# Row means of a binarized weight: reduced from its own layout on VectorE and spread through memory, in place of a product with ones

## The chip, the core and the metric

One core of one Trainium2 chip. The metric is the device time of one execution in microseconds (us), the median over several executions. The engines in the profile are PE (TensorE; PEld is its weight load), DVE (VectorE), ACT (ScalarE), POOL (GpSimd) and SP (SyncE, which here issues nearly all DMA transfers, in a fixed order).

## The reference, cut to what matters

A gated recurrence over 4096 time steps with a residual and a layer norm, then a feed-forward layer with binarized weights, a residual and a second layer norm. Only the second weight of the feed-forward layer is touched:

```python
# w1: (1024, 256)   w2: (256, 1024)   x: (2, 4096, 256)
def _binarize(w):
    alpha = mean(abs(w), axis=1, keepdims=True)
    return alpha * sign(w)          # forward value
h   = gelu(einsum('bsd,hd->bsh', x, _binarize(w1)) + b1)
out = einsum('bsh,dh->bsd', h, _binarize(w2)) + b2
```

So alpha of w2 is one number for each of the 256 output columns: the mean of the absolute values of 1024 weights. The kernel multiplies by the signs alone, and scales each output column by its alpha afterwards.

## The kernel before

The 4096 steps of each of the two sequences are cut into 64 segments of 64 steps that run side by side, each with 40 warm-up steps taken from the segment before it. One recurrence step is then one product of a 128x128 weight with 128 columns (`steps`, L165, PE) and one tanh (L170, ACT), and these steps follow one another strictly. The other work comes in 16 chunks of 512 rows: gates (L331), mix (L392, L399 to L407), projection (L417, L428), first layer norm, the two feed-forward products `up` (L514) and `down` (L563), second layer norm and store.

The whole order of work is written out by hand: within `tc.manual_schedule` each engine, SP included, runs its instructions in program order. Before the loop over chunks there is a start-up part, `for p in range(48)`: each `p` runs a part of the gates and lets a recurrence step in; `VISITS` puts in the products that make u (L138), which need the x tiles loaded by `load_xT` (L104); `AROUND` says after which `p` a load or a preparation of a weight is issued. `load_w(2)` and `load_w(3)` (p = 22 and 30) load the two halves of w2, `prepare_w(2)` and `prepare_w(3)` (p = 34 and 42) prepare them.

The layout of w2 in the chip is that of its transpose: `w2T` has h on the partitions (8 groups of 128) and the 256 output columns d in a row. `prepare_w` takes one half of it (4 groups) and does two things on DVE:

- the absolute values are summed over the 4 groups in one `tensor_reduce` through a rearranged view, 1024 values in and 256 sums out for each partition (L231); after the second half the two results are added (L239);
- the signs are formed (`signs`, L203 and L204) into `sg2`, the operand of `down`.

What is left is a sum over the 128 partitions. `mean_w2` (L246 to L250) does it after the start-up part, with one product of a 128x128 matrix of ones and the 256 sums (L248, PE). This also leaves the total in all 128 partitions, where `scale` (L579) needs it. DVE takes it out of PSUM with the factor 1/1024 into `al2_r` (L249). It uses a buffer `h` of pool `p_1` (three, shared with the gates' and `up`'s results), and `al2` takes one of three `hlo` buffers.

`mean_w2` stands right after the transposes of chunk 0 (`do(0, "turn", True)`) and ahead of `mix_end` of chunk 2, `norm` of chunk 1 and the last start-up gates. The first use of `al2_r` is `scale` of chunk 0, in the loop's round c = 1.

SP's order around these places is: ... x tile 2, half 2 of `w2T`, x tiles 3 and 4, half 3 of `w2T`, x tile 5, then the loads that chunks 0 to 2 need (`hu` from the state, `xn` from x, L364, L368, L373), then for chunk 3 `hu` (L364), an x tile for chunk 6 (L356), the other half of `hu` (L368) and `xn` (L373). After those come sixteen small transfers `xlo<-xb` for each chunk from 2 on (L480), which finish a transpose.

Of the kernel before, what the change touches and what calls it, by code (L numbers as in the profile page):

```python
# [8 lines left out]
FP = mybir.dt.float32  # L9
# [3 lines left out]
ALU = mybir.AluOpType  # L13
AX = mybir.AxisListType
PSUM = bass.MemoryType.PSUM

P = 128
B, T, DM, S, H = 2, 4096, 256, 64, 1024
KD = DM // P
# [4 lines left out]
N = 512  # L24
# [13 lines left out]
def gated_recurrence_then_binary_ffn(  # L38
# [9 lines left out]
    b_out: bass.AP,  # L48
    w1: bass.AP,
    w1T: bass.AP,  # L50
    w2T: bass.AP,
    b2: bass.AP,
    out: bass.AP,
):
    nc = tc.nc

    cp = ctx.enter_context(tc.tile_pool(name="const", bufs=1))
    xp = ctx.enter_context(tc.tile_pool(name="xin", bufs=2))
    wk = ctx.enter_context(tc.tile_pool(name="work", bufs=2))
    sm = ctx.enter_context(tc.tile_pool(name="small", bufs=4))  # L60
    p_s = ctx.enter_context(tc.tile_pool(name="p_s", bufs=1, space=PSUM))
    p_m = ctx.enter_context(tc.tile_pool(name="p_m", bufs=1, space=PSUM))
    p_1 = ctx.enter_context(tc.tile_pool(name="p_1", bufs=3, space=PSUM))
# [19 lines left out]
    b1_c = bias_c[:, 1 + KD :]  # L83
    bg_c = cp.tile([P, KD], FP, name="bg_c")
    al1 = cp.tile([P, KH], FP, name="al1")
    al2 = wk.tile([P, 2, DM], FP, tag="hlo", name="al2", bufs=3)
    bo_r = cp.tile([P, DM], FP, name="bo_r")
    b2_r = cp.tile([P, DM], FP, name="b2_r")
    al2_r = cp.tile([P, DM], FP, name="al2_r")
    ident = cp.tile([P, P], FP, name="ident")  # L90
    ones = cp.tile([P, P], FP, name="ones")
# [107 lines left out]
    def signs(dst, src, nm):  # L199

        for i in range(2):
            neg = wk.tile([P, N], FP, tag="xlo", name=f"neg{nm}_{i}")
            nc.vector.tensor_scalar(neg, src[:, bass.ts(i, N)], 0.0, None, ALU.is_lt)  # L203
            nc.vector.scalar_tensor_tensor(  # L204
                dst[:, bass.ts(i, N)], src[:, bass.ts(i, N)], 0.0, neg, ALU.is_gt, ALU.subtract
            )

    w_tiles = {}

    def load_w(n):  # L210
        half = bass.ts(n % 2, KH // 2)
        if n < 2:
            t = wk.tile([P, H], FP, tag="h", name=f"w1t{n}")
            nc.sync.dma_start(out=t, in_=w1T[:, n, :])
            t2 = wk.tile([P, KH // 2, DM], FP, tag="xhi", name=f"w1n{n}")
            nc.sync.dma_start(out=t2, in_=w1[:, half, :])
            w_tiles[n] = t, t2
        else:
            t = wk.tile([P, KH // 2, DM], FP, tag="h", name=f"w2t{n}")
            nc.sync.dma_start(out=t, in_=w2T[:, half, :])  # L220
            w_tiles[n] = t, None

    def prepare_w(n):
        half = bass.ts(n % 2, KH // 2)
        t, t2 = w_tiles[n]
        if n < 2:
            nc.vector.tensor_reduce(al1[:, half], t2, AX.X, ALU.add, apply_absolute_value=True)
            nc.vector.tensor_scalar(al1[:, half], al1[:, half], 1.0 / DM, None, ALU.mult)
            signs(sg1[:, n, :], t, f"a{n}")
        else:  # L230
            nc.vector.tensor_reduce(  # L231
                al2[:, n % 2, :],
                t.rearrange("p j d -> p d j"),
                AX.X,
                ALU.add,
                apply_absolute_value=True,
            )
            if n == 3:
                nc.vector.tensor_add(al2[:, 0, :], al2[:, 0, :], al2[:, 1, :])  # L239
            signs(  # L240
                sg2[:, half, :].rearrange("p j d -> p (j d)"),
                t.rearrange("p j d -> p (j d)"),
                f"b{n}",
            )

    def mean_w2():  # L246
        ps = p_1.tile([P, N], FP, tag="h", name="ps_al2")
        nc.tensor.matmul(ps[:, :DM], ones, al2[:, 0, :], start=True, stop=True)  # L248
        nc.vector.tensor_scalar(al2_r, ps[:, :DM], 1.0 / H, None, ALU.mult)  # L249
        yield  # L250


    class Stats:
# [430 lines left out]
    def ready():  # L684
        return done < len(plan) and plan[done] // SPC in have_u

    def next_steps():
        nonlocal done
        done += 1
        steps(plan[done - 1], done == WARM)  # L690
        for i in range(3):
            if done == WARM + (i + 1) * SPC:
                ch[i].load_h()
        if waiting and not held:
            for what, args in waiting:
                what(*args)
            waiting.clear()

    def emit(what, pieces, pace=5600):
        nonlocal since  # L700
        for _ in pieces:
            since += COST.get(what, 0)
            if since >= pace:
                since = min(since - pace, pace // 2)
                if ready():
                    next_steps()
# [5 lines left out]
    def do(i, what, *args, pace=5600):  # L712
        if not 0 <= i < len(ch):
            return
        if what == "load_h":
            need = WARM + (ch[i].c + 1) * SPC
            while done < need:
                next_steps()
            ch[i].load_h()
        elif what in ("load_u", "load_n", "load_x", "load_gate_x"):  # L720
            getattr(ch[i], what)()
        else:
            emit(what, getattr(ch[i], what)(*args), pace)
# [4 lines left out]
    def parts(n, pace):  # L728
# [10 lines left out]
        3: [(load_xT, 12), (load_xT, 13)],  # L739
        6: [(load_xT, 14)],  # L740
        8: [(load_w, 0)],
        11: [(load_xT, 15), (load_xT, 0)],
        13: [(load_weights,)],
        15: [(load_w, 1)],
        17: [(load_xT, 1)],
        18: [(prepare_w, 0)],
        20: [(load_xT, 2)],
        22: [(load_w, 2)],
        23: [(halve_weights,)],
        26: [(load_xT, 3), (load_xT, 4)],  # L750
        28: [(prepare_w, 1)],
        30: [(load_w, 3), (load_xT, 5)],
        34: [(prepare_w, 2)],
        36: [(ch[0].load_u,), (ch[1].load_n,)],
        40: [(ch[1].load_u,), (ch[2].load_u,)],
# [5 lines left out]
    with tc.manual_schedule(engines={ET.PE, ET.Activation, ET.DVE, ET.Pool, ET.SP}):  # L761
# [40 lines left out]
            next_steps()  # L802
        waiting = None
        do(0, "turn", True)
        emit("", mean_w2())
        mixed = ch[2].mix_end()
        next(mixed)
        do(1, "norm", nc.vector)
# [182 lines left out]
```

## Time and profile before

| | us |
|---|---|
| median of 3 runs (432.11, 432.14, 433.4) | 432.14 |
| time of the profiled execution | 432.98 |
| span from its first to its last instruction | 431.2 |
| first product of the start-up part's last visit to u (L138) | 52.63 |
| `mean_w2`'s product starts (L248) | 83.82 |
| `scale` first reads `al2_r` (L579) | 112.2 |

The mean granted clock of TensorE is 0.995 of full speed. A row of a timeline has the start, the time from the first start to the last end of the instructions merged in it, the engine (SPq is SP's queue), the line, the operation, the tiles (output, then inputs, without their numbers: `al` is al1 or al2, `al_r` is al2_r, `w2t` a half of w2T), the shapes and the number of instructions; in square brackets stands the engine's idle time before it and what ended it. A group's row has the shortest, median and longest duration in ns. A product of plain 32-bit floats shows as two PE instructions, so x2 is one product.

The first 65 us are the start-up part. The loop over chunks begins at about 86 us and ends at about 400; the last chunk's end follows.

### The profile page before, as it was taken

What the parts mean: (1) busy time and instruction counts of PE and PEld (TensorE: products, weight loads), DVE (VectorE), ACT (ScalarE), POOL (GpSimd) and SP (SyncE); (2) the same over time, 40 slices, a digit from 0 to 9 for tenths busy, and PEclk for the clock granted to TensorE, in tenths of its full rate; (3) what the DMA queues carried; (4) which work ended last, traced back from release to release, by engine and by line L of the source; (5) the groups of instructions that cost most, each with busy time, mean ns of one, the idle gap of its engine ahead of it and who ended that gap; (6) DMA issues with size and microseconds to landing.
All of it is one profiled execution on the core that took longest, in us unless ns stands there. A gap on an engine that the chain in (4) does not pass through costs nothing. (4 is left out here: it accounts for less than half of the span.)

```text
span 431.2 us, 6786 instructions
## 1 busy us (share of the span) xinstructions
PE 422.0 (98%) x2390; PEld 343.2 (80%) x2390; DVE 338.1 (78%) x570; ACT 282.7 (66%) x472; POOL 162.8 (38%) x176
## 2 busy tenths in 40 slices
PE   9999999999999999999999999999999999999992
PEld 6576767788888888887878787979797888889982
DVE  0254476996979797989898889889797979699784
ACT  3353533386586777777676767677767686849882
POOL 1000004474063444364625452535344444415513
PEclk9999999999999999999999999999999999999997
DMA  8785546000241625152515242524243232311102
GB/s 282 291 277 220 160 138 192 1 2 3 48 170 41 213 56 181 38 198 72 176 41 187 81 140 76 194 75 147 71 118 101 56 114 47 123 38 50 49 2 103
DMA packets 31047, 49.24 MB, mean 114 GB/s; under 512 B 5280, under 2 KB 19872, under 8 KB 31008
## 3 DMA queue, kind: packets, MB, share of 16 engines
q1 hardware_dynamic: 30432, 48.39, 35.4%
q8 instruction: 21, 0.34, 0.3%
q10 hardware_dynamic: 576, 0.37, 0.3%
q14 instruction: 18, 0.15, 0.1%
HBM read 29.33 MB, written 8.39 MB: 87 GB/s over the span
## 5 line engine op out<-in xcount | busy, mean ns | idle before, releaser
L563 PE MATMUL ps_o<-sg,hhi 128*128 128x256 f32 x488 | 118.3, 284 | 0.0
L563 PE MATMUL ps_o<-sg,hlo 128*128 128x256 f32 x488 | 115.1, 278 | 0.1
L524 ACT ACTIVATE h<-ps_h,bias_c,al 128x512 f32<-128x512 f32 x128 | 95.2, 771 | 14.8 <-PE ps_h L514 10.4
L377 POOL TENSOR_TENSOR xn<-xn,bo_r 128x256 f32<-128x256 f32 x64 | 58.0, 938 | 101.6 <-DMA xn<-in_x 98.6
L563 PEld LDWEIGHTS ps_o<-sg,hlo 128*128 128x128 f32 x488 | 91.8, 188 | 1.6 <-DVE hlo L543 0.6
L563 PEld LDWEIGHTS ps_o<-sg,hhi 128*128 128x128 f32 x488 | 91.9, 188 | 0.9
L514 PE MATMUL ps_h<-xhi,sg 128*128 128x512 f32 x256 | 92.3, 442 | 0.0
L543 DVE TENSOR_TENSOR hlo<-h,hhi 128x1024 fp32r<-128x1024 f32 (+1 forms) x65 | 82.5, 1289 | 4.0 <-ACT hhi L533 3.7
L514 PE MATMUL ps_h<-xlo,sg 128*128 128x512 f32 x256 | 79.6, 392 | 0.0
L533 ACT CAST hhi<-h 128x1024 fp32r<-128x1024 f32 (+1 forms) x65 | 67.4, 1039 | 2.0
L274 POOL TENSOR_TENSOR rs_b<-rs_b,neg_half 128x4 f32<-128x4 f32 (+1 forms) x17 | 28.2, 1658 | 104.8 <-DVE rs_b L273 99.9
L331 PE MATMUL ps_g<-xt,w_gate 128*128 128x384 f32 (+3 forms) x212 | 66.4, 426 | 0.0
L514 PEld LDWEIGHTS ps_h<-xhi,sg 128*128 128x128 f32 x256 | 46.4, 188 | 18.2 <-issue 10.0
L170 ACT ACTIVATE st<-ps_s 64x128 f32<-64x128 f32 x103 | 27.6, 268 | 46.4 <-PE ps_s L165 46.0
L377 POOL TENSOR_TENSOR xn<-xn,b_r 128x256 f32<-128x256 f32 x64 | 56.6, 913 | 1.1 <-PE ps_t L455 1.1
L514 PEld LDWEIGHTS ps_h<-xlo,sg 128*128 128x128 f32 x256 | 48.1, 188 | 10.9
L417 PE MATMUL ps_z<-w_out,tg 128*128 128x256 f32 x224 | 50.7, 379 | 0.0
L165 PEld LDWEIGHTS ps_s<-st,wab 128*128 128x128 f32 x208 | 35.7, 189 | 18.5 <-ACT st L170 9.2
L417 PEld LDWEIGHTS ps_z<-w_out,tg 128*128 128x128 f32 x224 | 41.5, 190 | 5.4 <-DVE tg L407 0.2
L488 ACT CAST xhi<-xlo 128x1024 fp32r<-128x1024 f32 x13 | 13.7, 1051 | 42.2 <-DMA xlo<-xb 36.4
L165 PE MATMUL ps_s<-st,wab 128*128 128x128 f32 x208 | 40.4, 276 | 0.0
L331 PEld LDWEIGHTS ps_g<-xt,w_gate 128*128 128x128 f32 x212 | 33.3, 192 | 7.2 <-issue 5.3
(86 smaller groups left out, 493.4 us busy)
## 6 DMA issues: line engine op xcount, KB each, us to landing
xt<-in_xT SPq DMA_DIRECT2D x31, 512.0 KB, 4.7
xn<-in_x SPq DMA_DIRECT2D x16, 512.0 KB, 3.2
out_y<-xn SPq DMA_DIRECT2D x15, 512.0 KB, 2.6
xlo<-xb SPq DMA_DIRECT2D x208, 32.0 KB, 1.9
hu<-st SPq DMA_DIRECT2D x32, 128.0 KB, 2.4
w1t<-in_w1T SPq DMA_DIRECT2D x2, 512.0 KB, 5.3
w1n<-in_w SPq DMA_DIRECT2D x2, 512.0 KB, 6.5
w2t<-in_w2T SPq DMA_DIRECT2D x2, 512.0 KB, 7.2
```

Of the source, the lines that this page charges most:

```text
L165: nc.tensor.matmul(p_h, ab, st[:, j].rearrange("p b k -> p (b k)"), start=True, stop=True)
L170: nc.scalar.activation(h_of[:, j + 1].rearrange("p b k -> p (b k)"), p_h[TOP, :], AF.Tanh)
L274: nc.gpsimd.tensor_tensor(rs, rs, neg_half[:, cut], ALU.pow)
L331: nc.tensor.matmul(ps[:, cut], w_gate[:, m, k, :], xt_[:, k, cut], start=k == 0 and i == 0, stop=k == KD - 1, skip_group_check=True,)
L377: nc.gpsimd.tensor_tensor(r[:, i, :], r[:, i, :], row, ALU.add)
L417: nc.tensor.matmul(self.ps_z[:, i, :], self.y[:, k, bass.ts(i, P)], w_out[:, k, :], start=k == 0, stop=k == KD - 1,)
L488: nc.scalar.copy(self.hi, self.lo.bitcast(FP))
L514: nc.tensor.matmul(ps, sg1[:, k, bass.ts(j, P)], part[:, k, :], start=n == 0, stop=n == 2 * KD - 1,)
L524: nc.scalar.activation(to, ps.rearrange("p (a i c) -> p a i c", a=P // 32, c=32) if self.far else ps, AF.Gelu, bias=b1_c[:, j : j + 1], sc ...
L533: nc.scalar.copy(hi[:, part, :], h[:, part, :])
L543: nc.vector.tensor_sub(lo[:, i, :], h[:, i, :], hi[:, i, :].bitcast(FP))
L563: nc.tensor.matmul(ps[:, i, :], part[:, j % 2, bass.ts(tb, P)], sg2[:, j, :], start=j == 0 and part is self.h[j // 2][0] and first, stop=j ...
```

## The change

w2 is loaded a second time in its own layout (new input `w2`: output column d on the partitions, in two groups of 128, and 1024 values of h in a row). The sum over h is then a plain reduction along the row, and gives a column of 128 means for each of the two halves. The 256 means are then brought into one row in every partition by two transfers: one writes the two columns (`al2`, 128 partitions x 2) to a scratch array in memory, and the other reads that array as a row of 256 into all 128 partitions of `al2_r`. The product with ones, its PSUM buffer and the instruction that took it out are gone. `al2` moves from the `hlo` buffers to a small constant tile, and the second load uses a `xhi` buffer, as the one for w1 does.

```diff
@@ load_w(n), n = 2, 3
             t = wk.tile([P, KH // 2, DM], FP, tag="h", name=f"w2t{n}")
             nc.sync.dma_start(out=t, in_=w2T[:, half, :])
-            w_tiles[n] = t, None
+            t2 = wk.tile([P, H], FP, tag="xhi", name=f"w2n{n}")
+            nc.sync.dma_start(out=t2, in_=w2[:, n - 2, :])
+            w_tiles[n] = t, t2
@@ prepare_w(n), n = 2, 3
-            nc.vector.tensor_reduce(
-                al2[:, n % 2, :],
-                t.rearrange("p j d -> p d j"),
-                AX.X,
-                ALU.add,
-                apply_absolute_value=True,
-            )
-            if n == 3:
-                nc.vector.tensor_add(al2[:, 0, :], al2[:, 0, :], al2[:, 1, :])
+            col = al2[:, n - 2 : n - 1]
+            nc.vector.tensor_reduce(col, t2, AX.X, ALU.add, apply_absolute_value=True)
+            nc.vector.tensor_scalar(col, col, 1.0 / H, None, ALU.mult)
...
-    def mean_w2():
-        ps = p_1.tile([P, N], FP, tag="h", name="ps_al2")
-        nc.tensor.matmul(ps[:, :DM], ones, al2[:, 0, :], start=True, stop=True)
-        nc.vector.tensor_scalar(al2_r, ps[:, :DM], 1.0 / H, None, ALU.mult)
-        yield
+    def spread_w2():
+
+        row = dp.tile([KD, P], FP, name="al2_d")
+        nc.sync.dma_start(out=row.rearrange("k p -> p k"), in_=al2)
+        nc.sync.dma_start(out=al2_r, in_=row.rearrange("k p -> (k p)").partition_broadcast(P))
...
         do(0, "turn", True)
-        emit("", mean_w2())
+        spread_w2()
         mixed = ch[2].mix_end()
```

Also changed: `al2 = cp.tile([P, KD], FP)`, a pool `dp` for the scratch array in memory, and the input `w2` made from `ffn_w2` on the host.

More of the change, by code (lines that the diff above doesn't have):

```diff
@@ L50, in gated_recurrence_then_binary_ffn @@
     w1T: bass.AP,
+    w2: bass.AP,
     w2T: bass.AP,
@@ L60, in gated_recurrence_then_binary_ffn @@
     sm = ctx.enter_context(tc.tile_pool(name="small", bufs=4))
+    dp = ctx.enter_context(tc.tile_pool(name="dram", bufs=1, space=bass.MemoryType.DRAM))
     p_s = ctx.enter_context(tc.tile_pool(name="p_s", bufs=1, space=PSUM))
@@ L85, in gated_recurrence_then_binary_ffn @@
     al1 = cp.tile([P, KH], FP, name="al1")
-    al2 = wk.tile([P, 2, DM], FP, tag="hlo", name="al2", bufs=3)
+    al2 = cp.tile([P, KD], FP, name="al2")
     bo_r = cp.tile([P, DM], FP, name="bo_r")
@@ L974 @@
         "w1T": rows(v["ffn_w1"].T, KD),
+        "w2": rows(v["ffn_w2"], KD),
         "w2T": rows(v["ffn_w2"].T, KH),
```

## The prediction

> **What bounds the kernel now.** I read the page's busy times and slices first:
>
> ```profile
> PE 422.0 (98%) x2390; PEld 343.2 (80%) x2390; DVE 338.1 (78%) x570; ACT 282.7 (66%) x472; POOL 162.8 (38%) x176
> ...
> PE   9999999999999999999999999999999999999992
> ...
> DVE  0254476996979797989898889889797979699784
> ```
>
> PE is full in every slice but the last (10.8 us each), while DVE is a third busy in the start-up part (slices 2 to 6). A busy PE might still be stalled in between, so the second view is the list of who waited for whom, for the weight loads:
>
> ```profile
> PEld ps_s L165 <- ACT st L170: 9.2, 28, 0.5
> ...
> PEld ps_h L514 <- ACT h L524: 0.9, 4, 0.2
> ...
> PEld ps_t L455 <- DVE xn L298: 0.2, 1, 0.2
> ```
>
> The columns are total us, times, longest. In the start-up part PE waits for the tanh of each recurrence step, so the strict chain of steps sets the pace there. Later PE waits for hardly anything: its own products set the pace. So DVE work in the start-up part is worth nothing unless it grows past DVE's gaps, and PE work after 65 us is worth its length as long as the engines that feed PE move with it.
>
> The third view is the timeline around `mean_w2`, first PE's, then DVE's, then the weight loads':
>
> ```profile
> 83.82 0.60 PE L248 MATMUL ps_al<-al,ones 128*128 128x256 f32 x2
> 84.25 1.47 PE L331 MATMUL ps_g<-xt,w_gate 128*128 128x128 f32 x8
> ```
> ```profile
> 86.33 0.41 DVE L249 TENSOR_SCALAR al_r<-ps_al 128x256 f32<-128x256 f32 x1
> 86.66 1.44 DVE L404 SCALAR_TENSOR_TENSOR d<-tg,d 128x1024 f32<-128x1024 f32 x1
> 88.03 2.67 DVE L298 TENSOR_SCALAR xn<-xn,mv_a,rs_a 128x256 f32<-128x256 f32 x4
> ```
> ```profile
> 90.75 0.53 PEld L455 LDWEIGHTS ps_t<-ident,xn 128*128 128x128 f32 x5 [0.18 <-DVE xn L298]
> ```
>
> Here PE reaches the transposes of chunk 1 and waits 0.18 us for DVE's norm (L298), which stands two instructions behind L249. So DVE, not PE, gates that point.
>
> **The change part by part.**
>
> *The product with ones goes.* The next PE work starts at 84.25 instead of 83.82 because of it: 0.43 us of PE.
>
> *Its read-out goes.* L404 starts 0.33 us after L249 starts (86.66 - 86.33; the 0.41 us include an overlap). DVE is continuous from L404 to L298's end at 88.03 + 2.67 = 90.70. So L298 ends up to 0.33 us sooner. PE comes 0.43 sooner and waits 0.18 + 0.43 - 0.33 = 0.28 us there, and 0.33 remains. But L298 takes 0.83 us per block (median) here, against 0.40 at its shortest, while POOL adds rows from 86.28 to 90.21; POOL starts from a DVE result ahead of L249 and does not move. DVE work pulled 0.33 us deeper into that stretch runs at about 0.40/0.83 of full pace, worth 0.33 x 0.48 = 0.16. So the gain at 90.75 is 0.16 to 0.33; I take 0.2, as the slow rows are the nearest ones. Behind it ACT and DVE are fed by PE, so that they move with it, and PE waits for nothing long to the end: 0.2 us stays.
>
> *The reductions.* Before and after both read 1024 values per partition:
>
> ```profile
> L227 DVE TENSOR_REDUCE al<-w1n x2: 1219/1220/1220, 23.7 to 40.8; 128x4 f32<-128x1024 f32 x2
> L228 DVE TENSOR_SCALAR al<-al x2: 170/170/170, 25.0 to 42.0; 128x4 f32<-128x4 f32 x2
> L231 DVE TENSOR_REDUCE al<-w2t x2: 1930/1934/1939, 44.2 to 58.9; 128x256 f32<-128x1024 f32 x2
> ```
>
> Gone are 2 x 1.93 and one add of 0.43 (L239): 4.3 us. Added are two reductions along the row and two factors of 1/1024. The reduction to one sum has no row; its bounds are 1.22 (w1's, to four sums, along the row) and 1.93. I take 1.22 as it has the same direction, so 2 x (1.22 + 0.17) = 2.8, at most 4.2. DVE saves 0.1 to 1.5 us, worth nothing on the path: after the first half's signs DVE idles 6.32 us and after the second's 4.12 us, both times until PE. That idle time covers it; without it the saving would be the first rival below. [...]
>
> *The second load of w2,* 512 KB each right behind the halves of w2T, is issued by SP in about 0.43 us (the row of an x tile). It delays what stands behind it:
>
> ```profile
> GB/s 106 259 306 132 355 411 417 386 24 4 7 153 300 253 51 0 0 117 289 295 248 138 320 173 0 4 0 0 0 0 0 7 0 0 0 0 0 0 13 45
> ```
>
> These are slices of 2.25 us from 20 us on. The queue is full from 29 to 38, then empty until 44.7; loaded to 51, then empty to 58. At about 400 GB/s each load adds 1.3 us. x tiles 3 and 4 then land by about 40 instead of 38, and are first read at 52.63. x tile 5 lands by about 53 instead of 51 and is read in that visit's last products, after 56.2. The reductions find their data too: they run at 44.2 and 58.9, data there by 40 and 53. Cover: 12 us and 3 us; if the second were gone, PE would wait for x tile 5 one to one.
>
> *The two transfers.* In program order they stand on SP behind the `hu` loads of chunks 1 and 2 and ahead of chunk 3's four loads:
>
> ```profile
> 61.53 3.98 SPq L368 DMA_DIRECT2D hu<-st  x2
> 67.53 0.48 SPq L364 DMA_DIRECT2D hu<-st  x1
> ...
> 69.47 0.58 SPq L373 DMA_DIRECT2D xn<-in_x  x1
> 106.16 3.96 SPq L480 DMA_DIRECT2D xlo<-xb  x6
> ```
>
> The write can go at 65.5: its input is ready when DVE has the second column, about 60.3. The read has to wait on SP until the write has landed. No row shows 256 runs of 4 bytes. From below 1.9 us (a 32 KB `xlo` transfer, issue to landing), from above 9.9 (the slowest x tile, in a full queue); the read is like the `b_r` row, 5.0, with the same bounds. I take 2.4 (`hu` rows, also narrow) and 5.0: `al2_r` is in place at about 73, at the latest at 85.3 (65.5 + two times 9.9). Its first reader is L579 at 112.2: 27 us of cover at worst. Queued behind the held read are chunk 3's `hu` (two), the x tile of chunk 6 and chunk 3's `xn`, 2 to 10 us later than at 67.5 to 69.5. POOL reads that `xn` at 101.84, PE that `hu` at 106.4, and chunk 6 comes later; with 3.2 us for landing they have 20 us to spare at worst. The sixteen `xlo` transfers come at 106.16. So nothing is paid. [...]
>
> *Buffers.* One `hlo` and one PSUM `h` buffer are free sooner, but their next users wait for neither now. Two more `xhi` buffers in a ring of two leave every later tile in its old place.
>
> Sum: -0.2 us, so 432.98 becomes about 432.8 in an execution like the profiled one (span 431.2 to 431.0); the profiled one lies 0.84 above the median. For the median: 432.14 - 0.2 = 431.9, with 431.8 to 432.2 as the limits of this case alone (0.33 gained, nothing gained, rounded up).
>
> **The rivals.**
>
> *DVE's saving counts.* If the start-up part were held by DVE, 1.5 us and the 0.33 at most would come off: 430.3. Against it: idle times of 6.32 and 4.12 us right behind. 0.06.
>
> *Slower by a shift of addresses.* In the built program the new constant tile moves all large tiles behind it 32 bytes on, from multiples of 64 bytes to 32 beyond. No row of before shows whether transfers or reads mind. The place would be the transposes' transfers: ACT waits 36.4 us in total for `xlo` to land, 11 times, about 3.3 each, and 13 chunks go through it. Each 0.1 us more per chunk costs up to 1.3 us; it decides once a landing grows by 0.1 (of 1.9) beyond the slack that PE has on ACT, which the 0.9 us of waits in total show to be thin. At 0.2 us: 432.14 - 0.2 + 2.6 = 434.5. Against: the same bytes in the same runs. 0.10.
>
> *SP is held.* The write would have to take 30 us (65.5 to 96, then 2.5 to issue chunk 3's loads and 3.2 to land) before POOL's L377 at 101.84 came late, at most one to one: 35 us would give 431.9 + 5 = 437. For it: the element-wise write has no row. Against: no landing above 9.9 us in this trace. 0.03. The change doing something else than it says is the same in time: PE has one product less, SP four transfers more.
>
> **How the numbers follow.** About 0.3% (1.3 us, 430.8 to 433.4) is what a measurement can tell from no change. Forecast 0.78; DVE's saving 0.06; addresses 0.10; SP held 0.03; 0.03 left for other delays. Faster: 0.06 and 0.01 of the forecast's noise, 0.07. Slower: 0.10 + 0.03 + 0.03 = 0.16. Same: 0.77. Predicted: 431.9. The range runs from 431.0 to 434.5: the forecast and the smaller half of the addresses' case.
>
> **What would show it.** L248 and L249 gone; the product after the transposes of chunk 0 and L404 0.3 to 0.4 us sooner; PE's wait before the transposes of chunk 1 longer than 0.18; DVE's idle time in the start-up part longer by about 1.5 in all; the read of `al_d` landing before 85.3; L579 waiting for PE as before. Wrong if PE waits for x tiles near 52 to 56, if ACT's waits for `xlo` grow past 36.4, or if chunk times after 110 us differ at all.

## The result, and the profile after

| | before | after |
|---|---|---|
| median, us | 432.12 (4 runs, 431.88 to 433.4) | 437.18 (4 runs, 437.09 to 437.36) |
| time of the profiled execution, us | 432.98 | 437.11 |
| span of it, us | 431.2 | 435.3 |

The changed kernel is slower by 5.06 us between the medians; the ratio is 1.0111, with an interval of 1.0091 to 1.0131. In the changed kernel the lines behind `spread_w2` have numbers lower by two (L402 is what was L404), and those of the recurrence steps numbers higher by two (L167 is what was L165).

The page of after, its first lines and two rows of the slices:

```profile
span 435.3 us, 6791 instructions
...
PE 426.1 (98%) x2388; PEld 346.2 (80%) x2388; DVE 333.8 (77%) x570; ACT 283.3 (65%) x472; POOL 155.2 (36%) x176
...
PE   9999999999999999999999999999999999999992
...
DVE  0255367995979797979797888888797979699684
```

PE has two instructions fewer (x2388 for x2390, the product with ones) and is busy for 4.1 us more. The share of 98% and the full slices look as they did, so this table alone doesn't tell a PE that waits less from one that works slower. The waits of the weight loads in after (us in total, times, longest):

```profile
PEld ps_s L167 <- ACT st L172: 9.3, 28, 0.5
...
PEld ps_h L512 <- ACT h L522: 0.5, 2, 0.2
PEld ps_t L453 <- DVE xn L296: 0.5, 2, 0.3
```

Against before these are +0.1, -0.4 and +0.3 us. No wait has appeared that would be worth 4 us. So the added time lies in the products themselves, and the groups of the page show in which. Before (busy us, mean ns of one, then idle time before it):

```profile
L563 PE MATMUL ps_o<-sg,hhi 128*128 128x256 f32 x488 | 118.3, 284 | 0.0
L563 PE MATMUL ps_o<-sg,hlo 128*128 128x256 f32 x488 | 115.1, 278 | 0.1
...
L514 PE MATMUL ps_h<-xhi,sg 128*128 128x512 f32 x256 | 92.3, 442 | 0.0
...
L417 PE MATMUL ps_z<-w_out,tg 128*128 128x256 f32 x224 | 50.7, 379 | 0.0
```

After:

```profile
L561 PE MATMUL ps_o<-sg,hhi 128*128 128x256 f32 x488 | 121.4, 287 | 0.0
L561 PE MATMUL ps_o<-sg,hlo 128*128 128x256 f32 x488 | 118.2, 281 | 0.0
...
L512 PE MATMUL ps_h<-xhi,sg 128*128 128x512 f32 x256 | 93.4, 446 | 0.0
...
L415 PE MATMUL ps_z<-w_out,tg 128*128 128x256 f32 x224 | 50.8, 380 | 0.0
```

The products of `down` (976 instructions; 48 more of the last chunk stand in other rows) are 3 ns longer on average and those of `up` (512, of which the rows with `xhi` are shown) 3 to 4 ns; the projection, which is a product of plain 32-bit floats, is hardly longer (380 for 379 ns). These durations include the overlap of one product with the next (284 ns on average in `down` before, while the weight loads of two products start 114.7 ns apart), so the time that a product really takes up on PE is better read from the distance between the starts of two weight loads that follow one another in the same kind of product. Worked out from the trace between 85 and 425 us (of those from 100 to 150 ns in `down`, 150 to 300 in `up` and 150 to 250 in the projection; the longer ones, where something came between, and a few of about half the length are left out), its mean is:

| | before | after |
|---|---|---|
| `down` (256 columns) | 114.7 ns | 117.9 ns |
| `up` (512 columns) | 230.2 ns | 233.9 ns |
| projection, one of a product's two instructions | 215.7 ns | 216.0 ns |

976 x 3.2 ns + 512 x 3.7 ns = 3.1 + 1.9 = 5.0 us: about the whole loss of 5.06 us. It should then grow over the whole loop, and it does, in steps that aren't quite even. The two executions of which there are traces differ by 4.13 us only, as that of before lies 0.86 us above its median. The start of `scale` on DVE in every second chunk, and at last in the last one, after minus before:

| at (us) | 112 | 156 | 200 | 244 | 289 | 333 | 377 | 420 |
|---|---|---|---|---|---|---|---|---|
| later by (us) | -0.22 | -0.07 | 0.58 | 1.72 | 2.05 | 3.24 | 4.03 | 4.05 |

The same in a view that counts: a window of the loop, with its length, the busy us (and instructions) of PE, PEld, DVE, ACT and POOL, PE's granted clock, DMA share and GB/s. Before, then after:

```profile
200.00:300.00 100.00, 100.00 (x566) 83.64 (x565) 87.60 (x148) 72.16 (x112) 44.75 (x46) 1.00 0.39 117
```
```profile
200.00:300.00 100.00, 100.00 (x556) 83.04 (x555) 84.25 (x144) 69.69 (x108) 40.10 (x44) 1.00 0.38 112
```

PE is busy for all of the 100 us in both, at the full granted clock in both, and starts 10 products fewer in after. The clock is not the cause; its mean over a whole execution lies between 0.993 and 0.997 in every run of this document.

### The profile page after: what moved, and what is told of

It is laid out like the page before. It is cut to its first block, busy times and chain, and to the rows that moved or that the text cites. A ratio compares the mean times of both kernels' runs of the same rounds, so it can differ in the third digit from the quotient of the medians.

```text
span 435.3 us, 6791 instructions
## 1 busy us (share of the span) xinstructions
PE 426.1 (98%) x2388; PEld 346.2 (80%) x2388; DVE 333.8 (77%) x570; ACT 283.3 (65%) x472; POOL 155.2 (36%) x176
## 4 chain that ended last, share of the span: by engine, by line
PE 96%; DVE 2%; POOL 0%; ACT 0%; issue 0%; POOLq 0%; DVEq 0%
PE ps_h L512 27%; PE ps_o L561 27%; PE ps_z L415 13%; PE ps_g L329 12%; PE ps_y L390 6%; PE ps_s L167 5%; PE ps_u L140 4%; PE ps_s L163 1%; PE ps_t L453 1%; DVE xn L296 1%; DVE d L402 0%; PE ps_p L561 0%; PE ps_q L561 0%; DVE xlo L463 0%; POOL xn L583 0%; DVE bs_b L262 0%
## 5 line engine op out<-in xcount | busy, mean ns | idle before, releaser
L561 PE MATMUL ps_o<-sg,hhi 128*128 128x256 f32 x488 | 121.4, 287 | 0.0
L561 PE MATMUL ps_o<-sg,hlo 128*128 128x256 f32 x488 | 118.2, 281 | 0.0
L512 PE MATMUL ps_h<-xhi,sg 128*128 128x512 f32 x256 | 93.4, 446 | 0.0
L375 POOL TENSOR_TENSOR xn<-xn,bo_r 128x256 f32<-128x256 f32 x64 | 53.2, 866 | 99.6 <-DMA xn<-in_x 90.5
L541 DVE TENSOR_TENSOR hlo<-h,hhi 128x1024 fp32r<-128x1024 f32 (+1 forms) x65 | 81.6, 1272 | 3.7 <-ACT hhi L531 3.6
L375 POOL TENSOR_TENSOR xn<-xn,b_r 128x256 f32<-128x256 f32 x64 | 53.6, 866 | 1.1 <-PE ps_t L453 1.1
L167 PEld LDWEIGHTS ps_s<-st,wab 128*128 128x128 f32 x208 | 35.8, 189 | 18.8 <-ACT st L172 9.3
L167 PE MATMUL ps_s<-st,wab 128*128 128x128 f32 x208 | 40.4, 276 | 0.0
L486 ACT CAST xhi<-xlo 128x1024 fp32r<-128x1024 f32 x13 | 13.6, 1050 | 38.8 <-DMA xlo<-xb 24.1
```

Source lines behind the costliest of these rows:

```text
L167: nc.tensor.matmul(p_h, ab, st[:, j].rearrange("p b k -> p (b k)"), start=True, stop=True)
L375: nc.gpsimd.tensor_tensor(r[:, i, :], r[:, i, :], row, ALU.add)
L512: nc.tensor.matmul(ps, sg1[:, k, bass.ts(j, P)], part[:, k, :], start=n == 0, stop=n == 2 * KD - 1,)
L541: nc.vector.tensor_sub(lo[:, i, :], h[:, i, :], hi[:, i, :].bitcast(FP))
L561: nc.tensor.matmul(ps[:, i, :], part[:, j % 2, bass.ts(tb, P)], sg2[:, j, :], start=j == 0 and part is self.h[j // 2][0] and first, stop=j ...
```

## Experiments

After the result there were two theories. *Addresses:* the eight bytes of `al2` per partition take 32 bytes among the constant tiles, ahead of `bo_r`; all tiles that are made later, those of the chunks among them, then lie 32 bytes further on within a stretch of 256 bytes, while `sg1` and `sg2`, which are made earlier, stay; the products of `up` and `down` have one operand on either side of that place, and mind. *Work:* one of the things that the change does (the additional loads, the transfers through memory, the product that is gone, the order of the buffers, since the `hlo` buffers are now made behind `hhi` rather than ahead of other tiles) disturbs the loop.

In the built kernels the place of `sg1` and `sg2` leaves 128 when divided by 256 (55936 and 64128), that of the chunk tiles 192 before and 224 after. Below, "distance" is the place of the chunk tiles minus that of the signs, in bytes by 256: 64 before, 96 after. The weights and the streamed columns of `down` are a part of `hhi` or `hlo` and of `sg2`; those of `up` are a part of `sg1` and of `xhi` or `xlo`. Medians, ratios with their 95% intervals and mean distances between weight loads of all runs stand in one table behind the experiments.

**1. The whole change, with `al2` back in an `hlo` buffer.** No tile moves against before.

```diff
-    al2 = cp.tile([P, KD], FP, name="al2")
+    al2 = wk.tile([P, KD], FP, tag="hlo", name="al2", bufs=3)
```

> All of the change is kept (second load, reductions, two transfers), but the small al2 is taken from the hlo buffers again, as before: no tile stands at another address than before. Theory A (the 32-byte shift of all later tiles slows every fp32r product by some 4 ns, 1488 of them, about 5 us): 431.7 us, gap between weight loads of down back at 113 to 114 ns. Theory B (the hlo buffers now lie behind the hhi buffers instead of ahead of the tg buffers): also 431.7. Theory C (the transfers, the loads or the missing buffer waits slow the loop): stays at 437.

Measured: 432.45 us beside 432.45 of before, ratio 1.0002. All loads, reductions and transfers of the change are in it and cost nothing. The theory of work falls, but for the order of the buffers, which is here as it was before.

**2. The change, with `al2` made 256 bytes long.** The order of the buffers is the change's; by 256 all later tiles have the same remainders as before.

```diff
-    al2 = cp.tile([P, KD], FP, name="al2")
+    al2 = cp.tile([P, 64], FP, name="al2")[:, 0:KD]
```

> The change, with al2 padded to 256 bytes per partition: every later tile is at a multiple of 64 bytes again (same remainder by 256 as before), while hlo stays behind hhi as in the changed kernel. Theory A (32-byte remainder): 431.7 us. Theory B (order of the buffers): 437. Theory C (the work itself): 437.

Measured: 432.49 us, ratio 1.0000. So the order of the buffers costs nothing either, and a shift by 256 bytes is as good as none: `down` is at 114.7 ns and `up` at 230.3 again.

**3. Before, with 32 unused bytes behind `al1`.** Nothing of the change but the shift.

```diff
     al1 = cp.tile([P, KH], FP, name="al1")
+    pad = cp.tile([P, 8], FP, name="pad")
...
+    nc.gpsimd.memset(pad, 0.0)
```

> The kernel before with one unused tile of 32 bytes per partition ahead of bo_r (and a memset of it on POOL): the same work, the same order of buffers, all later tiles 32 bytes on. Theory A: 432.1 + 5.4 = 437.5 us with the weight loads of down 117 to 118 ns apart. Theories B and C: 432.1.

Measured: 436.95 us, ratio 1.0104, and the same two distances between weight loads as in after, 117.9 and 233.9 ns. The groups of its page (numbers of lines higher by two than in before):

```profile
L565 PE MATMUL ps_o<-sg,hhi 128*128 128x256 f32 x488 | 121.4, 287 | 0.0
L565 PE MATMUL ps_o<-sg,hlo 128*128 128x256 f32 x488 | 118.1, 281 | 0.0
L516 PE MATMUL ps_h<-xhi,sg 128*128 128x512 f32 x256 | 93.4, 446 | 0.0
```

These are after's rows within 0.1 us. 32 bytes that nobody uses make the whole loss.

**4. The change, with `al2` made 64 bytes long** (as in 2, with 16 in place of 64): the chunk tiles are at multiples of 64 bytes again.

> The change with al2 padded to 64 bytes: later tiles at multiples of 256 bytes (before: remainder 192, a multiple of 64). Theory A in its form 'multiples of 64 are enough': 431.7 us, as the 256-byte padding. In the form 'the further aligned the faster': below 431. Theories B and C: 437.

Measured: 436.97 us, ratio 1.0107, so a multiple of 64 bytes isn't what matters, and neither form of the theory of addresses foresaw it. (That theories B and C say 437 here too doesn't bring them back: experiments 1 to 3 stand against both.) `down` is slower still (118.6 ns), `up` nearly as before (230.8): the two don't follow the same curve.

**5. Before, with 32 bytes ahead of `sg1`.** Signs and chunk tiles move together: if the place of the chunk tiles counts, this is as slow as 3; if the distance counts, it is as fast as before.

```diff
+    pad_a = cp.tile([P, 8], FP, name="pad_a")
     sg1 = cp.tile([P, KD, H], FR, name="sg1")
```

> The kernel before, with an unused 32-byte tile (and its memset) ahead of sg1: the two sign tiles and all tiles behind them move by 32 bytes together, so their distance stays as before (64 by 256) while each one's own remainder changes (tiles 192 to 224, signs 128 to 160). Theory R (what counts is the distance between the weight that is being loaded and the columns that are being read): about 432.3 us, weight loads of down 113 to 114 ns apart. Theory S (what counts is the remainder of the tiles themselves): 437 us, 117 to 118 ns.

Measured: 432.67 us, ratio 1.0004. The distance counts, not the place.

**6. Before, with the signs alone moved by 32 bytes** (32 ahead of `sg1`, and 224 behind `al1`, so that the chunk tiles move by 256): distance 32.

> The kernel before, with 32 bytes ahead of sg1 and 224 behind al1: the sign tiles move by 32, all later tiles by 256, so their remainders by 256 stay as before and only the distance to the signs falls from 64 to 32. Theory R: another time than before, by some us either way (the direction isn't known for this distance). Theory S: 432.3 us.

Measured: 436.59 us, ratio 1.0091, with the chunk tiles at places that 2 showed to be good ones. Moving the one operand is as bad as moving the other.

**7. Before, with 128 and with 192 bytes behind `al1`** (32 and 48 floats), distances 192 and 0.

> The kernel before, with 128 unused bytes behind al1: tiles at remainder 64 by 256, distance to the signs 192. If only the remainder by 128 counts: 432.3 us, as before. If by 256: another time, about 437 if every other remainder is slow.

> The kernel before, with 192 unused bytes behind al1: tiles and signs have the same remainder by 256 (128). Theory R in the form 'equal remainders collide': the slowest of all, over 437 us. Theory S, multiples of 64 of any kind: not decided by the runs so far; with 128-byte periods it is as the 64-byte padding, 437.

Measured: 435.49 and 436.69 us. A remainder by 128 is therefore not enough. Equal remainders (distance 0) are among the worse places for `down`, 119.0 ns, but not the slowest of all, which they would be if equal remainders collided: the runs at 96 and 128 lie at 436.95 to 437.18 us.

**8. The change, with `al2` made ahead of `sg1`.** Signs and chunk tiles move together, with all of the change in place.

```diff
+    al2 = cp.tile([P, KD], FP, name="al2")
     sg1 = cp.tile([P, KD, H], FR, name="sg1")
...
-    al2 = cp.tile([P, KD], FP, name="al2")
```

> The change whole, with al2 still a tile of 8 bytes, but declared ahead of sg1: signs and tiles move by 32 bytes together, distance 64 as before. Theory R: 0.2 us under before as the prediction had it (bounds 0 to 0.4), ratio 0.9990 to 1.0000. Were the distance not the cause: 437 us.

Measured: 432.67 us beside 432.75, ratio 0.9998, interval 0.9985 to 1.0011. One line of code in another place takes the loss away. The change as such is then worth nothing that can be measured, either way. The window of the loop, and the row of the products of `down` with `hhi` (shortest, median and longest ns, first and last start):

```profile
200.00:300.00 100.00, 100.00 (x570) 84.10 (x569) 87.75 (x147) 72.11 (x112) 46.43 (x45) 1.00 0.39 117
```
```profile
L561 PE MATMUL ps_o<-sg,hhi x488: 276/276/382, 96.0 to 419.3; 128*128 128x256 f32 x163
```

**9. Before, with `sg2` alone moved by 32 bytes** (32 between `sg1` and `sg2`, 224 behind `al1`): distance 32 for `down`, 64 as before for `up`.

> The kernel before, with 32 unused bytes between sg1 and sg2 and 224 behind al1: only the moving columns of down (sg2) change their distance to its weights (64 to 32); the weights of up (sg1) keep theirs. Theory R, pair by pair: weight loads of down 117 to 118 ns apart, those of up as before (about 230); 976 x 4 ns = some 4 us, 436. If instead any moved tile slowed all products: up slower too.

Measured: 435.05 us, ratio 1.0063. Its rows of `hhi` and `xhi`, and the same two rows of before and of after:

```profile
L567 PE MATMUL ps_o<-sg,hhi x488: 277/280/388, 96.0 to 421.7; 128*128 128x256 f32 x163
...
L518 PE MATMUL ps_h<-xhi,sg x256: 387/392/795, 85.3 to 417.9; 128*128 128x512 f32 x128
```
```profile
L563 PE MATMUL ps_o<-sg,hhi x488: 276/276/387, 96.8 to 419.6; 128*128 128x256 f32 x163
...
L514 PE MATMUL ps_h<-xhi,sg x256: 387/392/798, 86.1 to 415.6; 128*128 128x512 f32 x128
```
```profile
L561 PE MATMUL ps_o<-sg,hhi x488: 277/280/384, 96.4 to 424.0; 128*128 128x256 f32 x163
...
L512 PE MATMUL ps_h<-xhi,sg x256: 388/396/797, 85.3 to 420.3; 128*128 128x512 f32 x128
```

The medians: `down` at 280 as in after, `up` at 392 as in before. So each of the two kinds of product goes by its own pair of tiles. `up` has its usual pace with 256 bytes more between its two tiles.

**10. Before, with 96 and with 160 bytes behind `al1`** (24 and 40 floats), distances 160 and 224, for the places that were left.

> The kernel before, with 96 unused bytes behind al1: distance 160 by 256. Theory R says only that it differs; the distances so far: 0 436.7, 32 436.6, 64 432.6, 96 437.0, 128 437.0, 192 435.5. A plain rule (64 alone is good): 436 to 437. A mirrored rule (good at 64 and again at 160 to 192): 432 to 435.

> The kernel before, with 160 unused bytes behind al1: distance 224 by 256. A plain rule (64 alone is good): 436 to 437. A mirrored rule (a good place on the other side as well): 432 to 435.

Measured: 438.12 and 435.67 us. Neither of the two rules gives both: the first is above what the plain one says and far from the mirrored one, the second lies between them. All runs in the order of the distance; the sum is 976 and 512 times the additional ns against before, worked out as above, and "ratio" is against the executions of before taken with it (432.12 to 432.75):

| run | distance | median, us | ratio and interval | `down`, ns | `up`, ns | sum, us |
|---|---|---|---|---|---|---|
| before, 192 more (7) | 0 | 436.69 | 1.0109 [1.0078, 1.0140] | 119.0 | 230.7 | 4.4 |
| before, signs moved (6) | 32 | 436.59 | 1.0091 [1.0074, 1.0108] | 118.1 | 232.7 | 4.6 |
| before, `sg2` moved (9) | 32 / 64 | 435.05 | 1.0063 [1.0047, 1.0079] | 118.1 | 229.8 | 3.1 |
| before | 64 | 432.12 | | 114.7 | 230.2 | |
| change, `al2` in `hlo` (1) | 64 | 432.45 | 1.0002 [0.9991, 1.0013] | 114.7 | 230.3 | 0 |
| change, `al2` 256 bytes (2) | 64 | 432.49 | 1.0000 [0.9990, 1.0011] | 114.7 | 230.3 | 0 |
| before, all moved (5) | 64 | 432.67 | 1.0004 [0.9994, 1.0013] | 115.0 | 230.0 | 0.1 |
| change, `al2` ahead (8) | 64 | 432.67 | 0.9998 [0.9985, 1.0011] | 115.1 | 230.1 | 0.3 |
| after | 96 | 437.18 | 1.0111 [1.0091, 1.0131] | 117.9 | 233.9 | 5.0 |
| before, 32 more (3) | 96 | 436.95 | 1.0104 [1.0087, 1.0121] | 117.9 | 233.9 | 5.0 |
| change, `al2` 64 bytes (4) | 128 | 436.97 | 1.0107 [1.0091, 1.0124] | 118.6 | 230.8 | 4.1 |
| before, 96 more (10) | 160 | 438.12 | 1.0128 [1.0112, 1.0143] | 119.4 | 233.1 | 6.0 |
| before, 128 more (7) | 192 | 435.49 | 1.0067 [1.0051, 1.0084] | 116.9 | 232.9 | 3.5 |
| before, 160 more (10) | 224 | 435.67 | 1.0073 [1.0057, 1.0088] | 117.3 | 232.2 | 3.5 |

The sums follow the medians within about 1 us and are mostly a little above them. Of the eight distances the kernel before has the best, and every other one costs 0.7 to 1.3%. No version that was run is faster than before by more than the noise.

## Why the prediction was wrong

*The step that failed* is "Buffers", which cost the new place of `al2` at nothing and stands in the sum with no term for the constant tile that moves the chunk tiles. The rival "Slower by a shift of addresses" named the 32 bytes, but placed them at the transposes' transfers and priced them at 0.2 us a chunk; it got 0.10 of the chances, and its 434.5 was half the loss. The place is PE: 0.3 us for each chunk from 112 to 420 us (4.27 us over the 15 steps from one chunk to the next), on the engine that has no slack at all (busy for 100.00 of the 100 us from 200 to 300), 1488 times 3 to 4 ns. At the place that the rival named the opposite happened. The wait of ACT in after:

```profile
ACT xhi L486 <- DMA xlo<-xb: 24.1, 8, 4.3
```

It fell from 36.4 us and 11 times, and a transfer took 1.9 us to land in both. All of ACT's idle time ahead of that line fell less, from 42.2 to 38.8 us, as another engine was what it waited for last more often. Of the prediction's own signs of being wrong only the last one came: the times of the chunks after 110 us differ. The mistake in method was to look for the price of a shifted address only where waits are seen. A product of `down` that takes 3% longer (117.9 for 114.7 ns) made no wait (those of the weight loads changed by +0.1, -0.4 and +0.3 us); it had to be bounded by the busiest rows, and 1% of PE's 422 us is already 4.2 us.

*The product with ones* came off PE as said. In after:

```profile
82.51 1.04 PE L453 MATMUL ps_t<-ident,xn 128*128 128x128 f32 x8
83.38 1.47 PE L329 MATMUL ps_g<-xt,w_gate 128*128 128x128 f32 x8
```

All of after is 0.44 us early at this point (the transposes of chunk 0 start at 82.51 for 82.95). The gates' products come 0.87 us sooner than at 84.25, so 0.43 is gained.

*The 0.2 us that should remain of it* did not. DVE's and the weight loads' timelines of after:

```profile
85.89 1.79 DVE L402 SCALAR_TENSOR_TENSOR d<-tg,d 128x1024 f32<-128x1024 f32 x1
87.61 2.65 DVE L296 TENSOR_SCALAR xn<-xn,mv_a,rs_a 128x256 f32<-128x256 f32 x4
```
```profile
89.99 0.14 PEld L453 LDWEIGHTS ps_t<-ident,xn 128*128 128x128 f32 x1 [0.33 <-DVE xn L296]
90.31 0.53 PEld L453 LDWEIGHTS ps_t<-ident,xn 128*128 128x128 f32 x5 [0.18 <-DVE xn L296]
```

L402 starts where L249 stood (85.89 is 86.33 less the 0.44), 0.33 us sooner as predicted, but takes 1.79 us in place of 1.44. So L296 starts no sooner than before, relative to the rest, and PE waits 0.33 + 0.18 us: the last loads start at 90.31 for 90.75, the same 0.44 us early. Both durations of that line lie beside POOL's four additions (L377 before, L375 after), and it is with these that DVE keeps step: `norm` starts 1.75 us after their start before (88.03 - 86.28) and 1.76 after (87.61 - 85.85), and 1.74 to 1.76 us in experiments 1, 2, 3 and 8, whether 0.41 + 1.44 us stand ahead of it or 1.77 to 1.79. The prediction had POOL staying in its place, which was right, but took half of full pace for work that is pulled beside it; the runs show that work ahead of `norm` there is worth nothing. What couples DVE to POOL there isn't shown.

*The reductions.* The rows of `al2` in after (`al`, shortest, median and longest ns):

```profile
L236 DVE TENSOR_REDUCE al<-w2n x2: 1215/1218/1220, 44.0 to 58.6; 128x1 f32<-128x1024 f32 x2
L237 DVE TENSOR_SCALAR al<-al x2: 155/155/155, 45.2 to 59.9; 128x1 f32<-128x1 f32 x2
```

1.22 and 0.16 us, as taken. The time saved, 4.30 - 2.75 = 1.5 us, went into idle time, 6.84 and 5.11 us where it was 6.32 and 4.12, with PE no sooner for it. The rival "DVE's saving counts" fell with that.

*The second loads* fill the queue as worked out. GB/s in slices of 2.25 us from 20 us on in after: full to 38 and again from 44.7 to 53, where the forecast had 40 and 53.

```profile
GB/s 140 280 280 206 386 417 404 415 100 4 7 224 246 328 193 0 0 145 316 277 256 5 0 0 38 237 257 113 0 0 0 7 0 0 0 0 0 0 15 58
```

*The two transfers.* SP's queue in after, and their time from issue to landing (KB each, median us):

```profile
65.35 0.54 SPq L247 DMA_DIRECT2D al_d<-al  x1
73.20 0.33 SPq L248 DMA_DIRECT2D al_r<-al_d  x1
73.62 0.49 SPq L362 DMA_DIRECT2D hu<-st  x1
...
75.38 0.57 SPq L371 DMA_DIRECT2D xn<-in_x  x1
```
```profile
al_r<-al_d SPq DMA_DIRECT2D x1, 128.0 KB, 5.2
al_d<-al SPq DMA_DIRECT2D x1, 1.0 KB, 7.8
```

The write of 256 runs of 4 bytes took 7.8 us, inside its bounds of 1.9 and 9.9 but far from the 2.4 taken. The row of `hu` (128 KB in 2.4 us) was no measure for 1 KB in runs of 4 bytes. The row is in place at 78.4 us (73.20 + 5.2), not 73, and is first read at 112.0. Chunk 3's loads went out 6 us later (73.62 to 75.38 for 67.53 to 69.47), inside the 2 to 10 us worked out, and PE and POOL came to them as in before: POOL's additions of chunk 3 start at 101.24 (101.84 before), PE's products with `hu` at 106.11 (106.42). That "SP is held" had no ground is shown by experiment 1 too, which has the same transfers and before's time. Two figures on the way are off without touching the sum: DVE is about half busy, not a third, in the slices 2 to 6, and the smallest margin of chunk 3's loads is 19 us, not 20 (101.84 - 69.47 - 10 - 3.2).

## What to carry to other kernels

In this kernel, whose PE is full (98% of the span), a small tile added ahead of large ones was a change of its own: 32 unused bytes cost 1.04% (experiment 3). So look whether the distance between the two operands of the costly products stays, and compare the mean of a product in the page's groups before and after, since the 3 to 4 ns each made no wait here. To learn what a change is worth, measure it once with all addresses kept (the new tile last, padded, or ahead of both operands). Here a loss of 1.1% (5.06 us), spread over a loop which the edit doesn't touch, had such a cause.

## What was not expected of the hardware

The pace of the products of `up` and `down`, whose weights are loaded while the product before is running (from 200 to 300 us in before, PE is busy for 100.00 and its weight loads for 83.64), depends on the distance between the two operands' addresses: 114.7 to 119.4 ns for 256 columns (4.1%) and 229.8 to 233.9 for 512 (1.8%), at a granted clock of 0.993 to 0.997 throughout. A shift by 256 bytes left it as it was where that was run (experiment 2, 114.7 and 230.3 ns; for `up` also experiment 9, 229.8 ns). It has its best place at 64 of the eight distances tried (114.7 and 230.2 ns before), and differs between `down`, where the weights are the chunk tile, and `up`, where they are the signs: 128 and 0 cost `up` next to nothing (230.8 and 230.7 ns) and `down` 4 ns (118.6 and 119.0 ns). The projection, whose two operands (`tg` and `w_out`) also lie on either side of the shifted place, kept 215.7 to 216.0 ns in all runs, although the distance of these two (64 in before, `w_out` in its place) took all of the eight values but 32; it is a product of plain 32-bit floats, made of two instructions (as the one product of L248 was, x2).

These runs show a pace that depends, by up to 4.1% of a product (114.7 to 119.4 ns), on where the two operands lie; whether reads of the one hold up reads of the other isn't shown. Nor do the runs tell whether the distance that counts is that of a product's own two operands or that of the next weights and the columns still streaming, as all tiles of a kind have the same remainder. The same distance lies between the signs that PE reads and the chunk tiles that other engines work on at the time. That the work of DVE or POOL is the cause, the traces speak against: pairs of `down` loads around which both were idle (from 0.1 us before the first to 0.3 us after the second) are 113.8 ns apart in before (33 pairs) and 118.8 in after (53 pairs). ACT was busy around nearly all pairs, so its part isn't excluded. Not tried: distances finer than 32 bytes, other shifts by 256, and a product whose weights stay. Why 64 is the best place stays open.
